# Attention probabilities transposed by VectorE and DMA instead of TensorE, with the attention's instruction order written by hand, in a fused FFN-attention-FFN kernel

## The chip, the cores and the metric

The kernel runs on one core of a Trainium2 chip. The metric is device time in microseconds (us), the median of several runs. Engine names follow the profile: PE is TensorE's matmul side and PEld its weight loads, DVE is VectorE, ACT is ScalarE, POOL is GpSimd, and SP is the engine that issues the DMA transfers.

## The reference

All data are float32. The input `x` is 4 x 256 tokens of 512 features. Three layers are added to it in turn: half of a feed-forward layer of 64 gated low-rank experts, causal attention with 32 heads, and half of the feed-forward layer again. Each sees `x` normalized over its features.

```python
x = x + 0.5 * _L0_ffn_ref(_layernorm(x), A, B, Wr)
x = x + _L0_attn_ref(_layernorm(x), wq, wkv, wo)
x = x + 0.5 * _L0_ffn_ref(_layernorm(x), A, B, Wr)
```

The attention is what the change touches:

```python
q = einsum('bsd,de->bse', hidden, wq).reshape(B, S, 32, 192)
k, v = ...                                  # 32 heads of 128 each, from wkv
scores = einsum('bqhd,bkhd->bhqk', q[..., :128], k) * 192 ** -0.5
probs = softmax(where(causal, scores, -1e30), axis=-1)
attn = einsum('bhqk,bkhd->bqhd', probs, v).reshape(B, S, 32 * 128)
return einsum('bse,ed->bsd', attn, wo)
```

## The kernel before, in words

**Products with fewer multiplications.** Every large product is done by the Strassen-Winograd scheme, the attention's in two levels: an outer split into seven products M1 to M7, and each of these into seven again. Sums of operand blocks are made ahead: those of the weights by POOL (`two_levels`, with `right_sums` at line 187 and the outer sums at lines 588 to 609), those of the tokens once. One stage computes the seven inner products of one or two outer ones (`seven`, with the order in `STEPS`). Inner products M1, M6, M7 and M4 of a stage accumulate in one PSUM bank, M5 and M3 in a second, M2 in a third. After each product DVE or ACT reads the bank and adds it to its place in SBUF; M6 goes into the bank of M1 only when M1 has been read, and so on. Five banks (`ps_mm`) rotate among the stages.

**The attention.** The 32 heads form 16 pairs (`p`). While the units of pair `p` run, PE also computes q and k of pair `p + 1` (`make_qk`: stages a, b, c, d, e of M1, M2 with M6, M4 with M7, M5 and M3; matmuls at line 714, reads at 731 to 765) and part of v (`make_v`, every two pairs one set; matmuls at line 808, reads at 833 to 865). A unit is one head of one batch, so a pair has 8 and the kernel 128. Its work:
- `probs`: two score matmuls (lines 1084, 1085) into the one bank of `ps_s`. Causality leaves three blocks of 128 x 128: the first 128 queries against 128 keys, the second 128 against 256. DVE adds the mask and takes the row's extreme (1093), ACT takes the exponential with its row sum (1104), DVE the reciprocal (1112), and ACT scales (1114).
- `attend`: PE transposes the three blocks against an identity (1125), ACT copies them to SBUF as `pT` (1127), PE multiplies by v (1130, 1137), and ACT copies the result into `attn` (1144).

Unit u's `attend` runs in two halves under the next unit. Strings such as `"qvbqvbq"` (`UNITS`, `FIRST_UNITS`, `LAST_UNITS`) say how many steps of q (`q`), v (`v`), the attend halves (`b`) and the output projection (`o`) a unit takes. In pair 0 PE keeps exactly that order (`manual_schedule` of PE). In later pairs the strings give the order of recording, from which a scheduler of the language derives each engine's order. Which engine waits for what is always handled by semaphores. All DMA transfers are issued by SP, in order.

**Transfers around it.** `load_qk` and `load_v` bring the weights of later pairs in pieces of 128 KB (line 585) into rotating tiles, 7 for q and k and 6 for v. `sum_right` makes the operand sums of `wo` for a pair, `sum_left` those of `attn`; both go to DRAM (`kept_right`, `kept_left`; lines 570, 571, 925, 926). The output projection (`out_products`, 28 steps of 56 matmul instructions at line 1063, two for each product of 128 x 128 x 128) reads them back through tiles of three buffers (946, 956), makes the inner sums on DVE (975), and begins beside the units of the last pair. The second feed-forward layer follows.

Of the kernel before, what the change touches and what calls it, by code (L numbers as in the profile page):

```python
# [13 lines left out]
P = 128  # L14
# [6 lines left out]
HG = 2  # L21
# [11 lines left out]
def macaron_kernel(  # L33
# [16 lines left out]
        tc.tile_pool(name="scratch", bufs=1, space=bass.MemoryType.DRAM)  # L50
    )
# [506 lines left out]
    raw, rights, turns = {}, {}, {}  # L558

    def sum_right(p):  # L560

        w = opool.tile([P, HG, 512], F32, tag="w", name=f"wo_{p}", bufs=1)
        nc.sync.dma_start(w, wo_v[:, p * HG : (p + 1) * HG, :])
        t = opool.tile([P, 3, 256], F32, tag="t", name=f"to_{p}", bufs=1)
        b = [w[:, k, n * 256 : (n + 1) * 256] for k in range(2) for n in range(2)]
        right_sums(nc.gpsimd, [t[:, i, :] for i in range(3)], *b, pinned=True)
        to = kept_right[p // 4][:, p % 4]

        def keep():
            nc.sync.dma_start(to[:, 0], w[:, 0, 256:512])  # L570
            nc.sync.dma_start(to[:, 1:4], t)

        return keep

    def two_levels(pool, bufs, name, blocks, pinned):

        t = {
            m: pool.tile([P, 7, P], F32, tag="w", name=f"{name}_{m}", bufs=bufs)  # L580
            for m in ("M1", "M5", "M2", "M3", "M6", "M4")
        }
        for m, k, n in (("M1", 0, 0), ("M5", 0, 1), ("M2", 1, 0), ("M3", 1, 1)):
            for i, view in enumerate(blocks(k, n)):
                nc.sync.dma_start(t[m][:, i : i + 3 : 2], view)

        def t3():
            return nc.gpsimd.tensor_tensor(t["M1"], t["M6"], t["M1"], ALU.subtract)

        def sums(pinned=pinned):  # L590
            first = nc.gpsimd.tensor_tensor(t["M5"][:, 0:4], t["M5"][:, 0:4], t["M1"][:, 0:4], ALU.subtract)
            if pinned:
                tc.keep_in_program_order(first)

            right = {}

            def inner(m):
                v = t[m]
                right[m] = right_sums(
                    nc.gpsimd, [v[:, i] for i in range(4, 7)], *(v[:, i] for i in range(4))  # L600
                )

            inner("M1")
            inner("M2")
            nc.gpsimd.tensor_tensor(t["M6"][:, 0:4], t["M3"][:, 0:4], t["M5"][:, 0:4], ALU.subtract)
            inner("M6")
            for m in ("M5", "M3"):
                inner(m)
            nc.gpsimd.tensor_tensor(t["M4"], t["M2"], t["M6"], ALU.subtract)

            right["M7"] = right["M1"]
            inner4 = {0: "M1", 1: "M5", 2: "M2", 3: "M3", 4: "M6", 5: "M7", 6: "M4"}
            right["M4"] = {m: t["M4"][:, i] for i, m in inner4.items()}
            return right, t3

        return sums

    def load_qk(p):

        if p < NG:  # L620
            rights["qk", p] = two_levels(
                qkpool,
                7,
                f"wqk_{p}",
                lambda k, n: [
                    view[:, 2 * k : 2 * k + 2, p * HG + n, 0:DN] for view in (wq_v, wk_v)
                ],
                p == 1,
            )()

    def load_v(k):

        if 2 * k < NG:
            raw["v", k] = two_levels(
                vpool,
                6,
                f"wv_{k}",
                lambda c, n: [
                    wv_v[:, 2 * c : 2 * c + 2, (2 * k + n) * HG + j] for j in range(HG)
                ],  # L640
                k == 1,
            )

    def sums_v(k, pinned=False):
        rights["v", k] = raw["v", k](**({"pinned": True} if pinned else {}))
        return rights["v", k]

    with ExitStack() as scope:
# [3 lines left out]
        load_v(0)  # L652
# [6 lines left out]
            aside=lambda: sums_v(0, True),  # L659
# [41 lines left out]
    def make_qk(p):  # L701
        if p >= NG:
            return
        right, t3 = rights["qk", p]
# [63 lines left out]
        if p == 0:  # L768
            turns["qk"] = t3
        yield from stage(("M1",), m1, "a")  # L770
        if p > 0:
            t3()
            yield from stage(("M2", "M6"), onto_copy(slice(0, 4, 3)), "b")
        else:

            yield from stage(("M2",), onto_copy(slice(0, 1)), "n")
            yield from stage(("M6",), onto(base), "o")
        yield from stage(("M4", "M7"), m47, "c")
        yield from stage(("M5",), onto(slice(2, 4)), "d")
        load_qk(p + 1)  # L780
# [13 lines left out]
    def v_stages(k):  # L794
# [3 lines left out]
        right, t3 = rights.get(("v", k)) or sums_v(k)  # L798
        u = 2 + 2 * (k % 2)
        if k == 0:  # L800
            turns["v"] = t3
            t3 = None

# [53 lines left out]
        def m47(part, adds, ps, r):  # L857
# [11 lines left out]
            "M1": stage(("M1",), m1, "a", t3),  # L869
# [10 lines left out]
    def make_v(p):  # L880

        k = p // 2
        if p % 2:
            yield from chain(*(v_by[k + 1][m] for m in ("M2M6", "M4M7") if v_by[k + 1]))
        else:
            yield from v_by[k]["M5"]
            load_v(k + 1)
            v_by[k + 1] = v_stages(k + 1)
            yield from v_by[k]["M3"]
            if v_by[k + 1]:  # L890
                yield from v_by[k + 1]["M1"]
# [14 lines left out]
    def keep_first(p):  # L906

        nc.sync.dma_start(kept_left[p // 4][:, p % 4, 0], attns[p][:, 0, 0:512])
        yield

    def sum_left(p):

        s = hold.tile([P, 3, 512], F32, tag="so", name=f"so_{p}", bufs=1)
# [20 lines left out]
    def out_products(stream):  # L934
# [109 lines left out]
        for _ in sums(0):  # L1044
            pass
# [276 lines left out]
```

## Time and profile before

| what | us |
|---|---|
| median of 3 runs | 1159.51 (1158.92 to 1160.22) |
| the profiled execution's own time | 1158.9 |
| its span, first to last instruction | 1157.1 |

The profile shows one execution. Its span is 1.8 us shorter than that execution's own time. The granted TensorE clock is full (1.0) throughout. A "group" in the profile is all instructions of one line, engine, operation and shape; its row gives the time the engine was busy with it, the mean duration of one in ns, and behind the second bar the idle time just before them and who ended it. A duration runs from start to end of one instruction, and neighbours overlap in the pipeline, so the place that an instruction takes is read from the distance between starts. Some further groups that later steps refer to:

| group | count | mean ns |
|---|---|---|
| PE 1125, transpose of 128 x 128 | 384 | 273 |
| PE 1130 / 1137, products with v, 256 / 128 columns | 256 / 256 | 384 / 274 |
| DVE 1093, mask and extreme, 256 / 128 columns | 128 / 128 | 420 / 290 |
| ACT 1104, exponential, 256 / 128 columns | 128 / 128 | 496 / 402 |
| ACT 1114, scaling, 256 / 128 columns | 128 / 128 | 495 / 403 |
| POOL 187, inner sums of q and k weights, 128 x 128 | 320 | 456 |

By stretches of the span: the first layer runs to about 127 us, projections and the 128 units to about 888 us, the output projection (which begins at 852 us, beside the last pair) to about 1040 us, and the second layer to the end.

### The profile page before, as it was taken

How to read it: one execution, taken by the hardware profiler on the slowest of the kernel's cores; microseconds unless marked ns; L12 is line 12 of the kernel's file. 1: busy time of each engine (PE TensorE's matmuls, PEld its weight loads, DVE VectorE, ACT ScalarE, POOL GpSimd, SP SyncE). 2: the span in 40 equal slices, each digit the busy share in tenths (PEclk: the TensorE clock that was granted, in tenths of full speed). 3: DMA queues.
4: the chain of work that ended last, by engine and by line, in shares of the span. 5: the costliest groups of instructions: out<-in, count | busy, mean ns of one | idle time of the engine just before them, and what ended most of it. 6: DMA issues, size and time to landing. Idle time of an engine off the chain costs nothing.

```text
span 1157.1 us, 20441 instructions
## 1 busy us (share of the span) xinstructions
PE 1147.0 (99%) x7164; PEld 1009.6 (87%) x7164; DVE 756.9 (65%) x2096; ACT 483.5 (42%) x1438; POOL 617.0 (53%) x866
## 2 busy tenths in 40 slices
PE   9999999999999999999999999999999999999998
PEld 6677888899999999999999999999989999995767
DVE  5544776666666667667657767666686887866432
ACT  4444334455555545555555555545553000106410
POOL 4715487778768868768849859858520000001120
PEclk9999999999999999999999999999999999999999
DMA  9101111213233142233233232322386998741001
GB/s 336 69 1 37 44 49 28 82 47 114 99 99 110 56 146 103 62 120 119 68 106 110 93 109 75 127 81 94 137 291 208 364 312 299 252 145 60 19 19 37
DMA packets 107414, 136.73 MB, mean 118 GB/s; under 512 B 7472, under 2 KB 77104, under 8 KB 105136
## 3 DMA queue, kind: packets, MB, share of 16 engines
q1 hardware_dynamic: 107312, 135.43, 34.9%
q8 instruction: 57, 0.93, 0.3%
q14 instruction: 45, 0.37, 0.1%
HBM read 91.36 MB, written 44.04 MB: 117 GB/s over the span
## 4 chain that ended last, share of the span: by engine, by line
PE 95%; DVE 2%; DMA 1%; ACT 1%; issue 0%; SPq 0%; DVEq 0%; ACTq 0%
PE po_M L1063 14%; PE pqk_c L714 8%; PE po_f L418 8%; PE ph_f L350 8%; PE pqk_b L714 8%; PE pa L1130 5%; PE ps L1085 5%; PE pqk_e L714 4%; PE pqk_d L714 4%; PE pv_c L808 4%; PE pqk_a L714 4%; PE pv_b L808 4%; PE ptp L1125 4%; PE pa L1137 2%; PE ps L1084 2%; PE pv_e L808 2%
## 5 line engine op out<-in xcount | busy, mean ns | idle before, releaser
L1104 ACT ACTIVATE s<-s,least 128x128 f32<-128x128 f32 (+1 forms) x256 | 114.8, 449 | 207.0 <-DVE least L1093 207.0
L380 POOL TENSOR_TENSOR hg_f<-hg_f,gate_f 128x512 f32<-128x512 f32 x32 | 33.5, 1058 | 299.9 <-ACT gate_f L305 191.4
L1063 PE MATMUL po_M<-or_M,ol_M 128*128 128x128 f32 x1568 | 178.6, 275 | 1.4 <-DVE or_M L975 1.3
L1063 PEld LDWEIGHTS po_M<-or_M,ol_M 128*128 128x128 f32 x1568 | 177.0, 192 | 2.1 <-DVE or_M L975 1.9
L187 POOL TENSOR_TENSOR wqk_M<-wqk_M 128x128 f32<-128x128 f32 x320 | 137.9, 456 | 9.7
L714 PE MATMUL pqk_c<-xop,wqk_M 128*128 128x256 f32 x448 | 114.4, 380 | 0.1
L1114 ACT ACTIVATE s<-s,arden 128x128 f32<-128x128 f32 (+1 forms) x256 | 102.5, 449 | 13.6 <-DVE arden L1112 12.6
L714 PE MATMUL pqk_b<-xop,wqk_M 128*128 128x256 f32 x420 | 106.3, 379 | 0.0
L731 DVE TENSOR_TENSOR qk<-qk,pqk_b 128x512 f32<-128x512 f32 x105 | 72.2, 688 | 39.8 <-PE pqk_b L714 38.8
L975 DVE TENSOR_TENSOR ol_M<-ol_M 128x512 f32<-128x512 f32 x112 | 77.7, 694 | 21.5 <-DMA ol_M<-left 19.6
L1093 DVE CUSTOM_DVE_ANT_0 s<-ps,mask 128x128 f32<-128x128 f32 (+1 forms) x256 | 81.2, 355 | 12.1 <-PE ps L1085 9.3
L731 DVE TENSOR_TENSOR qk<-qk,pqk_c 128x256 f32<-128x256 f32 (+1 forms) x112 | 59.6, 532 | 42.0 <-PE pqk_c L714 24.9
L714 PEld LDWEIGHTS pqk_c<-xop,wqk_M 128*128 128x128 f32 x448 | 79.2, 191 | 8.5 <-DVE qk L731 0.9
L1144 ACT COPY attn<-pa 128x256 f32<-128x256 f32 x128 | 47.6, 372 | 84.5 <-PE pa L1137 69.7
L731 DVE TENSOR_TENSOR qk<-qk,pqk_d 128x512 f32<-128x512 f32 x112 | 74.7, 684 | 11.8 <-PE pqk_d L714 8.1
L714 PEld LDWEIGHTS pqk_b<-xop,wqk_M 128*128 128x128 f32 x420 | 74.8, 191 | 7.4
L1130 PE MATMUL pa<-pT,vbuf 128*128 128x256 f32 x256 | 77.3, 384 | 0.5 <-ACT pT L1127 0.3
L1085 PE MATMUL ps<-qk 128*128 128x256 f32 x256 | 76.5, 380 | 0.0
L187 POOL TENSOR_TENSOR wv_M<-wv_M 128x128 f32<-128x128 f32 x160 | 69.0, 456 | 11.2 <-DMA wv_M<-in_wkv 4.8
L1127 ACT COPY pT<-ptp 128x384 f32<-128x384 f32 x128 | 60.1, 469 | 29.8 <-PE ptp L1125 28.9
L430 DVE TENSOR_TENSOR x<-x,po_f 128x256 f32<-128x256 f32 x56 | 23.5, 420 | 63.4 <-PE po_f L418 63.3
L714 PE MATMUL pqk_a<-xop,wqk_M 128*128 128x256 f32 x224 | 64.2, 381 | 0.5 <-ACT qk L738 0.5
(191 smaller groups left out, 2576.9 us busy)
## 6 DMA issues: line engine op xcount, KB each, us to landing
ol_M<-left SPq DMA_DIRECT2D x56, 512.0 KB, 5.6
left<-attn SPq DMA_DIRECT2D x15, 1024.0 KB, 3.9
left<-so SPq DMA_DIRECT2D x16, 768.0 KB, 5.1
wv_M<-in_wkv SPq DMA_DIRECT2D x64, 128.0 KB, 2.7
wqk_M<-in_wq SPq DMA_DIRECT2D x64, 128.0 KB, 2.3
wqk_M<-in_wkv SPq DMA_DIRECT2D x64, 128.0 KB, 2.7
wo<-in_wo SPq DMA_DIRECT2D x16, 512.0 KB, 3.9
or_M<-right SPq DMA_DIRECT2D x32, 256.0 KB, 5.7
```

The lines of the kernel that those rows point to most:

```text
L187: pieces = [lambda eng, of=of: eng.tensor_tensor(*of, ALU.subtract) for of in sums]
L350: nc.tensor.matmul(ps, lhsT=left[m][:, c, :], rhs=a_right[m][:, c, :], start=first and c == 0, stop=c == 1, skip_group_check=True,)
L418: nc.tensor.matmul(ps[:, 0:256], lhsT=left[m][:, c, :], rhs=b_right[m][:, c, :], start=first and c == 0, stop=c == 3, skip_group_check=True,)
L714: nc.tensor.matmul(ps[:, i * S : (i + 1) * S], lhsT=right[m][n], rhs=xop[OUTER[m]][:, INNER[n]], start=first and i == 0, stop=True, skip_g ...
L731: nc.vector.tensor_tensor(to, of, ps, ALU.add)
L808: nc.tensor.matmul(ps[:, i * S + t * P : i * S + (t + 1) * P], lhsT=xop[OUTER[m]][:, INNER[n], t * P : (t + 1) * P], rhs=right[m][n], star ...
L1063: nc.tensor.matmul(banks[at // 2][:, cols : cols + P], lhsT=left[n][:, g, t * P : (t + 1) * P], rhs=right[n][:, g], start=k % 4 == 0 and g ...
L1085: nc.tensor.matmul(ps[:, P : 3 * P], lhsT=qT[:, P : 2 * P], rhs=kT, start=True, stop=True)
L1093: nc.vector.tensor_tensor_reduce(out=s[:, cols], in0=ps[:, cols], in1=mask_f[:, cols], scale=-SCALE, scalar=-TAKEN, op0=ALU.add, op1=ALU.m ...
L1104: nc.scalar.activation(s[:, cols], s[:, cols], AF.Exp, bias=least[:, i : i + 1], scale=-1.0, accum_out=den[:, i : i + 1],)
L1114: nc.scalar.mul(s[:, cols], s[:, cols], rden[:, i : i + 1])
L1130: nc.tensor.matmul(po[:, 0 : 2 * P], lhsT=v_of(p, j, 2 * b), rhs=pT[:, 0 : 2 * P], start=True, stop=False,)
```

## The change

**The transposition.** For units 8 to 117 of the 128 the transposes leave PE. ACT writes its scaled probabilities to a PSUM tile `pn` whose columns are grouped so that the 32-column groups k = 0 to 3 of all three blocks lie together. One DVE instruction transposes every 32 x 32 block of it into `pb` in SBUF. That turns the elements inside each block, but each block still lies in the 32 partitions of its queries and not in those of its keys. Four DMA transfers (one per 32 partitions) write the blocks to a DRAM tile `moved`, in runs of 96 elements, and a fifth reads it back as `pT` with the keys in the partitions. The columns of `pT` are then in the order (q, t, c) of 4 x 3 x 32, and `attend` reads its moving operand through a rearranged view, in runs of 32. `attend` comes two units after `probs` (it was one). Pair 0 and the last ten units keep the transposes on PE (`turn`), with ACT's copy.

**The order.** From pair 1 to the end of the units, and for the first 54 of 392 steps of the output projection, the order on PE, DVE, ACT, POOL and SP is the order of recording. `merged` interleaves the steps of q and v in proportion to their PE time, `written` places a unit's parts at marks in estimated PE time, and tables (`Q_SUMS`, `V_SUMS`, `LEFT_SUMS`, `RIGHT_SUMS`, `Q_LOADS`, `V_LOADS`, `LEFT_STORES`) say in which unit which sums and transfers stand. The sums of a pair, made in one go before, are spread over the units. The left stores become seven transfers per pair. The first step of the output projection loads into free tiles of the q and k weights, during pair 14. The buffers of `s` go from 3 to 2.

The core of the diff:

```diff
-    def probs(h, b):
+    def probs(h, b, by_dma=True):
...
         nc.vector.reciprocal(rden, den)
+        if not by_dma:
+            for i, cols in enumerate(parts):
+                nc.scalar.mul(s[:, cols], s[:, cols], rden[:, i : i + 1])
+            pTs[h, b] = s
+            return
+        pn = ps_t.tile([P, 4, 3, 32], F32, tag="pt", name=f"pn_{n}")
         for i, cols in enumerate(parts):
-            nc.scalar.mul(s[:, cols], s[:, cols], rden[:, i : i + 1])
-        return s
...
+            nc.scalar.mul(
+                pn[:, :, i : 2 * i + 1, :].rearrange("p k t c -> p t k c"),
+                s[:, cols].rearrange("p (t k c) -> p t k c", k=4, c=32),
+                rden[:, i : i + 1],
+            )
+        yield
+        pb = work.tile([P, 4, 96], F32, tag="pb", name=f"pb_{n}", bufs=1)
+        nc.vector.transpose(pb.rearrange("p k c -> p (k c)"), pn.rearrange("p k t c -> p (k t c)"))
+        moved = turning.tile([P, 4, 96], F32, tag="moved", name=f"moved_{n}")
+        for q in range(4):
+            nc.sync.dma_start(
+                moved[:, q].rearrange("(k r) x -> r k x", r=32), pb[32 * q : 32 * q + 32]
+            )
+        yield
+        pT = pTs[h, b] = work.tile([P, 4, 3, 32], F32, tag="pT", name=f"pT_{n}")
+        nc.sync.dma_start(pT.rearrange("p q t c -> p (q t c)"), moved.rearrange("p q x -> p (q x)"))
...
+    def attend(h, b):
...
+        of = pTs.pop((h, b)).rearrange("p q t c -> p t q c")
...
-            rhs=pT[:, 0 : 2 * P],
+            rhs=of[:, 0:2],
...
-            rhs=pT[:, 2 * P : 3 * P],
+            rhs=of[:, 2:3],
...
+    ENGINES = {EngineType.PE, EngineType.DVE, EngineType.Activation, EngineType.Pool, EngineType.SP}
...
+    def classic(number):
+
+        return number < 8 or number >= 8 * NG - 10
+
+    def written(p, unit, steps, streams, transfers):
+
+        number = 8 * p + unit
+        made = probs(*units[number], not classic(number))
+        next(made)
+        todo = sums_of(p, unit)
+        t, done, n = 0.65, 0, len(todo)
+
+        marks = [(1.3, made), (1.9, pending.pop(0)), (2.0, transfers), (2.8, made)]
+        if not classic(number):
+            marks.append((4.2, made))
+        if not classic(number - 2):
+            marks.append((2.1, units[number - 2]))
+        if classic(number - 1):
+            marks += [(1.0, ("turn", *units[number - 1])), (2.2, units[number - 1])]
...
+        for i, (k, cost) in enumerate(steps):
+            take(streams[k], 1)
+            t += cost
+            while done < n and (done + 0.5) / n <= (i + 1) / len(steps):
+                todo[done]()
+                done += 1
+            while marks and marks[0][0] <= t:
+                t += mark(marks.pop(0)[1])
...
+            written_out.enter_context(tc.manual_schedule(engines=ENGINES))
```

The marks read: exponentials (1.3), the fifth transfer of the unit before (1.9), other transfers (2.0), `attend` of the unit two back (2.1), reciprocal and scaling (2.8), block transpose and four writes (4.2), in us of PE time from the unit's start; the score matmuls and DVE's reductions stand at its head.

## The prediction

> **What bounds the kernel now.** I read the page from the top: busy time by engine, then the chain that ended last.
>
> ```profile
> PE 1147.0 (99%) x7164; PEld 1009.6 (87%) x7164; DVE 756.9 (65%) x2096; ACT 483.5 (42%) x1438; POOL 617.0 (53%) x866
> ...
> PE 95%; DVE 2%; DMA 1%; ACT 1%; issue 0%; SPq 0%; DVEq 0%; ACTq 0%
> ```
>
> TensorE is busy for 99% of the span and carries 95% of the chain. A busy engine can hide waits, so I asked for the busy time in the stretch that the change rewrites, from the first projection products (127.6 us) to the end of pair 14.
>
> ```profile
> 127.60:836.00 708.40, 705.97 (x4399) 642.62 (x4398) 482.26 (x1346) 356.05 (x1137) 532.23 (x762) 1.00 0.28 92
> ```
>
> The columns are length, then busy time with instruction count of PE, PEld, DVE, ACT and POOL, then granted clock, DMA share and GB/s. PE is idle for 2.4 us of 708.4; DVE is busy 68%, ACT 50%, POOL 75%, DMA 28%. The transpose matmuls of line 1125 start between 153.3 and 885.8 us, one group per unit, so a unit (one head of one batch) takes 732.5/127 = 5.77 us on average. Work taken from PE here shortens the kernel one for one, unless something takes the freed place.
>
> **What is removed from PE.** The timeline of PE shows what the three transposes of a unit cost:
>
> ```profile
> 245.73 0.49 PE L1125 MATMUL ptp<-ident,s 128*128 128x128 f32 x3
> 246.06 1.06 PE L808 MATMUL pv_c<-wv_M,xop 128*128 128x128 f32 x8
> ```
>
> They look 0.49 us long, but the next matmul starts 0.33 us after the first one, so their place is 0.33 us. (The group's 63.0 us for 384 counts pipeline ends that lie under the next matmul.) Units 8 to 117 go by DMA, 110 of 128; pair 0 and the last ten keep the transposes. Gain: 110 x 0.33 = 36.3 us. Against the profiled execution of 1158.9 us (span 1157.1) that leaves 1122.6 us. The other matmuls stay the same in number and shape, but `attend` now reads its moving operand in runs of 32 columns. No row has such an operand. Low end 0; high end one more 128x128 pitch (0.11 us, a third of the 0.33) for each of 220 matmuls, 24 us. I take 0, because all contiguous rows move at the same rate per column and the run is still 128 bytes.
>
> **VectorE.** 110 block transposes of 128x384 are added.
>
> ```profile
> L731 DVE TENSOR_TENSOR qk<-qk,pqk_d 128x512 f32<-128x512 f32 x112 | 74.7, 684 | 11.8 <-PE pqk_d L714 8.1 <-POOL wqk_M L187 0.8 <-POOL qk L765 0.3
> L731 DVE TENSOR_TENSOR qk<-qk,pqk_e 128x256 f32<-128x256 f32 x112 | 45.4, 417 | 14.8 <-PE pqk_e L714 12.2
> L1127 ACT COPY pT<-ptp 128x384 f32<-128x384 f32 x128 | 60.1, 469 | 29.8 <-PE ptp L1125 28.9
> ```
>
> By the two DVE rows 128 columns cost (684 - 417)/2 = 134 ns, so 384 columns take 0.55 us, 0.47 back to back (such operations follow each other about 80 ns before the listed end). Low end 0.42 (the 256 row), high end 0.95 (two cycles per element). I take 0.47: 52 us of DVE. Per unit DVE has 3.93 us (68% of 5.77) and then 4.40 of 5.44, or 81%. ACT loses the 0.47 us copy and keeps its two scalings; POOL keeps 4.34 us per unit, or 80%. None becomes the bound on average.
>
> The average is not the limit, though. PSUM banks tie PE to DVE closely: in a stage of seven products, M1, M6, M7 and M4 use one bank, so the product after next waits until DVE has read the one before (`STEPS`). DVE runs in order, and two new waits stand in its hand-written order: the reciprocal behind ACT's exponentials (it was placed by the scheduler before) and the transpose behind ACT's scaling. Behind a waiting transpose are queued the reads of the next products, and PE waits for those within about one product, 0.43 to 0.86 us. The worst place is stage d (M5), where each product of 0.43 us brings a 128x512 read of 0.60. I counted the DVE order of the changed kernel in such a unit: two reductions 0.56, six reads of d at 0.60, reciprocal 0.1, transpose 0.47, one read of e 0.34: 5.07 us, beside PE's 7 x 0.43 + 2 x 0.44 + 2 x 0.65 = 5.2. It just fits, with nothing left for a wait on ACT. Low end of these waits 0; high end 0.7 us in each of the 28 such units, 20 us. I take 0.2 us in each: 6 us. They belong to the hand-written order as a whole; its other moves (sums spread over POOL, earlier loads) I cost at nothing, since POOL has 20% free. If that cover is gone, PE waits for weight sums directly.
>
> **SP and the DMA engines.** Each of the 110 units issues five more transfers: four writes of 32 partitions (128 runs of 384 bytes each) and one read of 128 rows of 1536 bytes. The left stores are also cut from two transfers per pair to seven.
>
> ```profile
> 532.50:538.50 6.00, 6.00 (x42) 5.59 (x41) 3.33 (x11) 3.74 (x13) 4.36 (x8) 1.00 0.49 134
> ```
>
> In this window six weight loads of 128 KB ran, each 256 runs of 512 bytes: 0.49 x 6.0 x 16 engines = 47 engine-us for 1536 runs, 31 ns a run. A unit's 512 written runs then take 512 x 31/16 = 1.0 us of all engines, the read about 128 x 61/16 = 0.5 us (61 ns for 1536 bytes, from 40 ns a KB in the window of the left stores at 542 to 551 us, where the share is 0.51). So the share rises from 28% by 1.5/5.44 = 28% to some 58%. Here the Trainium skill speaks against the change. "DMA: Bandwidth & Descriptors", Rules for kernel authors, says to transpose by the hardware's DMA transpose and not by a plain transfer with a rearranged pattern, which is 19 times slower; its Specifications say that below 512 bytes an engine reads, modifies and writes. By the first, the unit's 196 KB (0.7 us at the window's 134/0.49 = 273 GB/s) would take 14 us, far over the unit, and the kernel some 2000 us. I don't take it: VectorE has turned the elements already, and DMA only moves whole runs of 96. By the second the writes may double to 2.0 us and the share reach 76%, still under the unit. No run of before writes so short a run. I take the row, and the doubled price as the high end.
>
> The SP queue matters more, because it waits in order. The read of a unit waits on SP until its four writes have landed, and behind it stand the next unit's weight loads and left stores, and the next four writes. From the rows:
>
> ```profile
> right<-wo SPq DMA_DIRECT2D x16, 128.0 KB, 1.8
> ...
> 515.90 0.34 SPq L570 DMA_DIRECT2D right<-wo  x1
> ...
> 532.69 0.37 SPq L585 DMA_DIRECT2D wqk_M<-in_wq  x1
> 533.15 1.96 SPq L585 DMA_DIRECT2D wv_M<-in_wkv  x4
> ```
>
> The round is three issues at 0.34, then 1.8 us from the last issue to its landing (the nearest row: 128 runs to DRAM), the read's issue 0.38, and 22 other transfers per pair, 2.75 per unit at 0.44 = 1.2: in all 4.4 us of 5.44. Latency: from the transpose (4.2 to 4.9 us into unit n) about 1.0 + 1.8 + 0.2 + 2.6 (the landing of the small weight loads) = 5.6 us; the matmul that needs it stands 2.1 us into unit n + 2, some 7.5 us later. There are about 2 us to spare. Units with six or seven other transfers overrun by up to 1 us and get it back in the next. So I cost the round at nothing. Nobody else waits on it except ACT, through the `attn` buffer that a late left store keeps.
>
> **Last pair.** It stays as it was in kind, and its loads must still come: PE idled 1.7 us of 46 in 844 to 890, and after that has no idle time to lose although DMA is at 0.97. I take no change, within 3 us either way.
>
> **The rivals.**
> A, the likeliest: 1158.9 - 36.3 + 6 = 1128.6 us; with the 0.6 us by which the median of before lies over its profiled run, 1129. For it: 2.4 us of idle PE before, and room on every engine. Its own range is 1120 to 1137.
> B, VectorE's in-order waits cost more: 0.7 us in the 28 stage d units (20 us) and 0.05 us in all 110 (5 us), no more than is within reach of the 0.95 us price of a transpose. 1122.6 + 25 = 1148 us. For it: DVE at 97% of the unit in stage d. Against: before, at 68% load, PE stood only 0.6 us for reads of d.
> C, slower: the SP round. Place: the read's wait in SP for the writes' landing. If a short write lands in 3.5 us and not 1.8, the round is 6.1 us, PE waits for each pT, and 110 x (6.1 - 5.44) = 73 us come back: 1196 us. The point from which it decides: above 5.44 us a round it eats the gain, above 5.77 (landing over 3.1 us) the kernel is slower. For it: left<-attn landed in 3.9 us, and short writes may be dearer. Against: those were 1 MB, and the 128 KB store took 1.8.
> D, the gain is eaten in full: POOL, ordered by hand, delivers weight sums late; stage b, about 7 us into a pair, needs M6's sums, whose loads land some 3 us into the pair and then take 4.9 us. A delay of 2.6 us in each of 14 pairs gives 1159. Against: the first products of b need none of the inner sums.
>
> **How the numbers follow.** A 0.58, B 0.21, C 0.17, D 0.04. The predicted time is A's, 1129. The range takes in A and B with the uncertain ends, 1120 to 1158, and leaves out C, D and a little. Within 0.2% (about what a measurement of this kernel can tell from no change) lies D alone. A and B are faster, 0.79; D 0.04; C 0.17.
>
> **What would show it.** Right: PE instructions fewer by 330, PE still at 98% or more between 196 and the last pair, a unit of about 5.45 us, DVE near 80% there, waits of pqk_d and pqk_e products on DVE of some 6 us in all, almost none of the pa products on pT's load. Each block transpose should take 0.5 to 0.6 us. Wrong by C: pa products waiting for DMA in nearly every unit, and moved landing in over 3 us. Wrong by B: DVE waiting for ACT's pn, with PE waiting for DVE in the units of stage d. Wrong by D: pqk_b waiting for POOL. What would break the sum altogether: matmuls of pa that take longer than 379 and 274 ns.

## The result and the profile after

The changed kernel takes 1201.28 us in the median of 4 runs (1196.65 to 1207.47), the kernel before 1159.22 us in runs on the same chip (1158.72 to 1160.22). The ratio is 1.037, with a 95% interval of 1.032 to 1.041: slower by 42 us, where 1129 us was forecast. The profiled execution of the changed kernel took 1196.65 us, its span 1194.8 us.

The page of the kernel after, busy time by engine and then the chain that ended last:

```profile
PE 1133.5 (95%) x6834; PEld 981.5 (82%) x6834; DVE 792.3 (66%) x2230; ACT 443.6 (37%) x1328; POOL 619.5 (52%) x866
...
PE 34%; DMA 2%; DVE 2%; POOL 1%; SPq 1%; issue 1%; ACT 1%; DVEq 0%; POOLq 0%; ACTq 0%
```

TensorE (PE) lost the 330 instructions as planned (7164 to 6834), but it is idle for 61.3 us where it was idle for 10.1. The shares of the chain add up to under half, so I take from it only that DMA and SyncE's queue (SPq) have more of it than before. The rewritten stretch, from the first projection products to the end of pair 14, in the same columns as in the prediction (length, busy time of PE, PEld, DVE, ACT and POOL, granted clock, DMA share, GB/s):

```profile
128.00:866.00 738.00, 686.22 (x4058) 609.75 (x4057) 512.55 (x1454) 316.54 (x1029) 530.81 (x761) 0.99 0.51 144
```

PE is idle for 51.8 us of 738, where 2.4 of 708.4 were idle. No other engine is near full: DVE 69%, ACT 43%, POOL 72%, DMA 51%. Who PE waits for is in the list of its waits (us in total, times, longest):

```profile
PE pa L1234 <- DMA pT<-moved: 23.6, 16, 2.7
PE pqk_e L729 <- DVE qk L746: 13.8, 11, 2.1
PE pqk_d L729 <- DVE qk L746: 6.1, 13, 0.6
PE pv_b L821 <- POOL wv_M L610: 3.1, 5, 1.2
PE pqk_e L729 <- POOL vbuf L878: 2.8, 3, 0.9
```

The first row is the new transfer, the next two are reads of stages d and e. The groups that were added or priced in the prediction (by shape: line, engine, tiles, count, busy us, mean ns, then idle time before and its releaser):

```profile
L746 DVE TENSOR_TENSOR qk<-qk,pqk_d 128x512 f32<-128x512 f32 x112 | 73.0, 678 | 2.9 <-PE pqk_d L729 1.7 <-POOL wqk_M L610 0.2
...
L1203 DVE STREAM_TRANSPOSE pb<-pn 128x384 f32<-128x384 f32 x110 | 63.5, 578 | 40.2 <-DMA moved<-pb 37.6 <-ACT qk L753 2.3 <-ACT pn L1196 0.3
```

A block transpose takes 578 ns, as sized (0.55). Idle before it, 37.6 us, is DVE waiting until the writes out of the one `pb` buffer have landed. The transfers, with the median time from issue to landing, and what SyncE waited for:

```profile
moved<-pb SPq DMA_DIRECT2D x440, 48.0 KB, 2.3
pT<-moved SPq DMA_DIRECT2D x110, 192.0 KB, 2.5
```

```profile
SPq L1211 <- DMA moved<-pb: 171.5, 180, 3.2
```

In total, for 171.5 us a read of `pT` stood at the head of SyncE's queue and waited for the writes, and everything behind it waited too. How that looks in one unit of pair 7, first SyncE's queue, then PE:

```profile
568.31 0.34 SPq L1211 DMA_DIRECT2D pT<-moved  x1
568.70 2.99 SPq L607 DMA_DIRECT2D wv_M<-in_wkv  x6
571.73 0.47 SPq L950 DMA_DIRECT2D left<-attn  x1
572.30 1.90 SPq L1206 DMA_DIRECT2D moved<-pb  x4
576.04 0.34 SPq L1211 DMA_DIRECT2D pT<-moved  x1
```

```profile
575.72 0.61 PE L821 MATMUL pv_a<-wv_M,xop 128*128 128x128 f32 x4
578.72 0.67 PE L1234 MATMUL pa<-pT,vbuf 128*128 128x256 f32 x2 [2.39 <-DMA pT<-moved]
579.23 0.38 PE L1241 MATMUL pa<-pT,vbuf 128*128 128x128 f32 x2
579.45 1.62 PE L729 MATMUL pqk_c<-xop,wqk_M 128*128 128x256 f32 x4
```

The reads stand 7.73 us apart: seven other issues take 3.4 us, the four writes 1.9, then SyncE does nothing from 574.20 to 576.04 until the last write has landed. The read lands about 2.5 us later, and the product that needs it starts 2.39 us late. The four `pqk_c` products after it take 1.62 us where the same four took 1.03 at 574.85 us; that is the clock (last section).

### The profile page after: what moved, and what is told of

Its sections match the earlier page's. It is cut to its first block, busy times and chain, and to the rows that moved or that the text cites. A ratio compares the mean times of both kernels' runs of the same rounds, so it can differ in the third digit from the quotient of the medians.

```text
span 1194.8 us, 21108 instructions
## 1 busy us (share of the span) xinstructions
PE 1133.5 (95%) x6834; PEld 981.5 (82%) x6834; DVE 792.3 (66%) x2230; ACT 443.6 (37%) x1328; POOL 619.5 (52%) x866
## 5 line engine op out<-in xcount | busy, mean ns | idle before, releaser
L1134 PE MATMUL po_M<-or_M,ol_M 128*128 128x128 f32 x1512 | 172.3, 275 | 0.0
L1134 PEld LDWEIGHTS po_M<-or_M,ol_M 128*128 128x128 f32 x1512 | 171.0, 192 | 0.3
L610 POOL TENSOR_TENSOR wqk_M<-wqk_M 128x128 f32<-128x128 f32 x320 | 141.0, 456 | 12.1
L610 POOL TENSOR_TENSOR wqk_M<-wqk_M,wqk_M 128x512 f32<-128x512 f32 (+1 forms) x64 | 107.1, 1682 | 30.5 <-DMA wqk_M<-in_wkv 14.9
L1234 PE MATMUL pa<-pT,vbuf 128*128 128x256 f32 x256 | 78.8, 389 | 25.5 <-DMA pT<-moved 23.6
L1196 ACT ACTIVATE pn<-s,arden 128x128 f32<-128x128 f32 x220 | 93.8, 427 | 11.6 <-DVE arden L1188 7.5
L610 POOL TENSOR_TENSOR wv_M<-wv_M,wv_M 128x512 f32<-128x512 f32 (+1 forms) x32 | 53.8, 1680 | 76.2 <-DMA moved<-pb 32.5
L1203 DVE STREAM_TRANSPOSE pb<-pn 128x384 f32<-128x384 f32 x110 | 63.5, 578 | 40.2 <-DMA moved<-pb 37.6
L1037 DVE TENSOR_TENSOR ol_M<-ol_M 128x512 f32<-128x512 f32 (+1 forms) x112 | 74.6, 666 | 19.1 <-DMA ol_M<-left 16.5
L729 PE MATMUL pqk_e<-xop,wqk_M 128*128 128x256 f32 x224 | 64.8, 395 | 16.7 <-DVE qk L746 13.8
L780 POOL TENSOR_TENSOR qk<-qk 128x256 f32<-128x256 f32 x64 | 46.4, 727 | 58.4 <-DVE qk L746 58.3
```

The lines of the kernel that those rows point to most:

```text
L610: return nc.gpsimd.tensor_tensor(to, a, b, ALU.subtract)
L729: nc.tensor.matmul(ps[:, i * S : (i + 1) * S], lhsT=right[m][n], rhs=xop[OUTER[m]][:, INNER[n]], start=first and i == 0, stop=True, skip_g ...
L1037: nc.vector.tensor_tensor(of[:, :, to], of[:, :, a], of[:, :, b], op)
L1134: nc.tensor.matmul(banks[at // 2][:, cols : cols + P], lhsT=lhsT, rhs=rhs, start=k % 4 == 0 and g == 0 and at % 2 == 0 and t == 0, stop=Tr ...
L1196: nc.scalar.mul(pn[:, :, i : 2 * i + 1, :].rearrange("p k t c -> p t k c"), s[:, cols].rearrange("p (t k c) -> p t k c", k=4, c=32), rden[ ...
L1203: nc.vector.transpose(pb.rearrange("p k c -> p (k c)"), pn.rearrange("p k t c -> p (k t c)"))
```

## The experiments

**How the loss is divided.** The forecast less its 6 us for DVE is a span of 1157.1 - 36.3 = 1120.8 us. The starts of the projection's stage a tell where each kernel is later than that. Lengths of a pair in us, mean over pairs 2 to 13, worked out from the traces (the forecast row is the one of before less 8 x 0.33):

| kernel | even pairs | odd pairs |
|---|---|---|
| before | 43.9 | 47.0 |
| forecast with no new wait | 41.3 | 44.4 |
| after | 46.8 | 49.3 |
| e1 loads first | 46.3 | 46.7 |
| e3 no move | 41.9 | 46.6 |
| e4 order only | 44.6 | 48.7 |
| e7 spread | 44.1 | 46.8 |
| e10 best | 42.3 | 45.8 |

**The two halves of the change.** e4 keeps the written order and leaves all transposes on TensorE; e3 keeps the transposes on DVE and leaves out the five transfers.

```diff
 # e4
-        return number < 8 or number >= 8 * NG - 10
+        return True
 # e3
-        pb = work.tile([P, 4, 96], F32, tag="pb", name=f"pb_{n}", bufs=1)
+        pb = work.tile([P, 4, 96], F32, tag="pT", name=f"pb_{n}")
-        moved = turning.tile([P, 4, 96], F32, tag="moved", name=f"moved_{n}")
...
-        nc.sync.dma_start(pT.rearrange("p q t c -> p (q t c)"), moved.rearrange("p q x -> p (q x)"))
+        pTs[h, b] = pb.rearrange("p q (t c) -> p q t c", t=3)
```

> The changed kernel with the transposes on PE in all units, so only the order written by hand and the moved loads and sums remain. If the order costs nothing: 1156 to 1164 us, with PE idle of about 10 us as before. If the order costs waits of its own: 1170 us or more. SP's rounds do not exist here; both theories on the transfers say nothing.

> The changed kernel without the five transfers of a unit: VectorE's block transpose writes straight into pT and attend reads that, so the blocks are left in their queries' partitions. The output projection and all else stays. Left out: the move of the blocks between partitions. It measures the block transposes and the hand-written order alone. If SP's round and the transfers cause the whole loss: 1122 to 1135 us (36.3 us saved on PE, few waits). If VectorE's load or the order written by hand causes a good part of it: over 1150 us.

e4 took 1180.54 us (ratio 1.018, 1.017 to 1.020), e3 1145.68 (0.9885, 0.987 to 0.990). The written order alone costs 21 us; and e3, which leaves out the move of the blocks between partitions and so has none of its transfers, is 23 us above the 1122.6 of the sum. So this part of the loss does not need the transfers. That the two amounts agree does not show that they have one cause. PE's waits in stages d and e are 8.8 us in e4 and 14.0 in e3 (0.6 in the kernel before), first e4, then e3:

```profile
PE pqk_d L729 <- DVE qk L746: 5.3, 10, 0.6
PE pqk_e L729 <- DVE qk L746: 3.5, 8, 0.5
```

```profile
PE pqk_d L729 <- DVE qk L746: 7.2, 16, 0.6
PE pqk_e L729 <- POOL vbuf L878: 5.7, 6, 0.9
PE pqk_e L729 <- DVE qk L746: 1.1, 2, 0.9
```

The row with POOL is a wait for DVE too. At 524.86 us, for example, PE starts when DVE's read of `pqk_e` has ended (524.75), and that read stood behind a read that had waited 0.88 us for ACT's copy and behind the block transpose (523.83 to 524.41).

The rest, from e3 to the changed kernel (1194.8 - 1145.4 = 49.4 us of span, 55.6 by the medians), belongs to the transfers.

**The transfers: order of the issues.** e1 issues the other transfers of a unit before the read, so that the writes land under them; e2 gives `pb` a second buffer (and `s` one in place of two, for the space).

```diff
 # e1
-        marks = [(1.3, made), (1.9, pending.pop(0)), (2.0, transfers), (2.8, made)]
+        marks = [(1.3, made), (1.9, transfers), (2.0, pending.pop(0)), (2.8, made)]
 # e2
-        pb = work.tile([P, 4, 96], F32, tag="pb", name=f"pb_{n}", bufs=1)
+        pb = work.tile([P, 4, 96], F32, tag="pb", name=f"pb_{n}", bufs=2)
```

> The changed kernel with two marks exchanged: in each unit SP issues the weight loads and left stores (1.9) ahead of the read of pT (2.0). The theory is that SP's round per unit is the bound: four writes, wait for their landing, read, other transfers, 5.97 us from one read of pT to the next where PE needs 5.44. With this order the other transfers are issued while the writes land, about 1.26 us a unit comes off the round, which falls to some 4.7 us, below PE's unit. Then the waits of pa for pT and of DVE for pb go, and the kernel takes 1125 to 1145 us. The rival that the DMA engines themselves are too slow for these short runs, or that the hand-written order is at fault, expects 1185 to 1205 us, because neither the transfers nor the other engines' orders change.

> The changed kernel with two buffers of pb, at the cost of one of s (the units with transposes on PE keep their s in the pb buffers). It takes away DVE's 37.6 us of waiting for the landing of moved. If the SP round is the bound, the lateness only moves: pa waits longer for pT, the distance of the reads stays near 5.9 us, and the time stays at 1185 to 1205 us. If the loss comes from DVE standing behind a single buffer (in-order waits on DVE), the PE waits for reads of stages d and e (20 us) and their clock loss go, and it takes 1165 to 1175 us.

e1: 1176.11 us (1.015, 1.014 to 1.017), 25 us gained by exchanging two marks. e2: 1199.48 (1.035, 1.033 to 1.038): the buffer is not the cause, the lateness only moves (PE's wait for `pT` rises from 23.6 to 33.4 us). In e1 the odd pairs are as long as in e3 (46.7 and 46.6 us), so there the transfers cost nothing any more; the even ones lose 4.4 us each, and those are the pairs with one unit of seven and one of six other transfers.

e7b leaves the queue as it is and gives each round 2.5 us more time before its product; e7 exchanges the marks as e1 does, spreads the loads so that no unit has more than five other transfers, and has the later product too.

```diff
 # e7b and e7
-            marks.append((2.1, units[number - 2]))
+            marks.append((4.6, units[number - 2]))
 # e7 alone, besides the edit of e1
-    Q_LOADS = {6: ("M1", "M5"), 7: ("M2", "M3")}
-    V_LOADS = {3: ("M1", "M5", "M2"), 6: ("M3",)}
+    Q_LOADS = {5: ("M1",), 6: ("M5",), 7: ("M2", "M3")}
+    V_LOADS = {2: ("M1",), 3: ("M5",), 4: ("M2",), 6: ("M3",)}
```

> The changed kernel with one edit: the product pa of a unit stands at 4.6 us in the second unit after it instead of 2.1, so each transfer round has 2.5 us more. Theory that only the latency of single rounds with six or seven other transfers was too long: 1148 to 1160, pa waits nearly gone. Rival, that SyncE's rounds are on the average longer than a unit (5.97 us measured against 5.44), so that any slack is used up and lateness accumulates: 1185 to 1200, pa waits 15 us or more.

> Three edits that leave all work as it is: the other transfers ahead of the read (as e1), the weight loads spread so that no unit has more than five other transfers instead of seven, and pa at 4.6 us. If SyncE's bursts are all that e1 still loses over e3 (its even pairs lose about 4 us each at pa, the odd ones none): 1144 to 1152 us, no waits of pa on pT. If the transfers' own contention costs as well: 1155 to 1170.

e7b took 1207.06 us (1.041, 1.039 to 1.042). The wait for `pT` has all but gone, and the time has not. PE's waits in e7b:

```profile
PE pqk_d L729 <- DVE qk L746: 14.8, 17, 2.1
PE pqk_e L729 <- DVE qk L746: 12.3, 11, 2.7
PE pv_b L821 <- POOL wv_M L610: 7.3, 6, 1.8
PE pqk_a L729 <- POOL wqk_M L610: 6.9, 6, 1.2
...
PE pa L1234 <- DMA pT<-moved: 2.4, 6, 0.4
```

So it is the rate of SyncE's rounds, not their latency: with more time they take it through other doors, DVE waiting for `pb` (48.7 us) and POOL for late weights. The rate must be read with care. There is one read of `pT` per unit, so the distance of the reads is the length of a unit in every version, whatever holds it up (5.97 us in the changed kernel, 6.06 in e7b, 5.50 in e10). What tells is the round without the time in which SyncE stands at the writes until DVE has made the block transpose. Worked out from the traces, it is 5.46 us in the changed kernel and 5.32 in e7b, with nothing to spare against the forecast's unit of 5.44, but 4.13 in e1 and 4.12 in e10. In 59 of the changed kernel's 109 rounds SyncE goes on to the writes within 0.15 us.

e7, where the rate is mended, took 1160.00 us (1.000, 0.999 to 1.001), 47 us below e7b, but outside the 1144 to 1152 expected if bursts were all that was left. Of the 14 us by which it lies above e3, 5.9 are waits for `pT`, and PE's wait of `pqk_a` for ACT rose by 5.5 (0.7 to 6.2). That second wait is as long in e7b, which has only the later product, so the later product has a price of its own.

**The written order: the scheduler back.** e5, e5a, e5b and e5d take engines out of the set whose order is written by hand.

```diff
-    ENGINES = {EngineType.PE, EngineType.DVE, EngineType.Activation, EngineType.Pool, EngineType.SP}
+    ENGINES = {EngineType.PE, EngineType.SP}
 # e5 with e4's edit; e5b alone; e5d with e1's edit
+    ENGINES = {EngineType.PE, EngineType.DVE, EngineType.Pool, EngineType.SP}
 # e5a, with e4's edit
```

> All transposes on TensorE as in e4, and only TensorE's and SyncE's order written by hand; VectorE, ScalarE and GpSimd are ordered by the scheduler again. Theory (the hand order of the three vector engines makes VectorE late in stages d and e and costs some 20 us): 1159 to 1164 us, pqk_d and pqk_e waits on DVE under 3 us. Rival 1 (TensorE's new order, the placing of scores, turns and products among the projection steps, is what costs): 1178 to 1183, as e4. Rival 2 (SyncE's order of the ordinary transfers makes POOL's sums late): 1175 or more with the waits on POOL and wqk/wv tiles.

> As e4 (all transposes on TensorE, order by hand), except that ScalarE alone is ordered by the scheduler. If the cost of the hand order is that ScalarE's copies of stage c stand behind scalings and exponentials, and VectorE waits for them in order (qk of line 746 on ACT line 777, 65.5 us in e4, 16.1 in the kernel before): 1159 to 1166, that wait back near 20 us. If VectorE's own order is to blame (its reads stand behind the softmax rows and the reciprocal): 1176 to 1182.

> The changed kernel with only TensorE's and SyncE's order by hand, the vector engines ordered by the scheduler. If the two costs add (about 22 us for the order of the vector engines, about 55 us for SyncE's round of transfers): 1176 to 1184 us, the waits of pa on pT still 20 us or more. If SyncE's round hides what the vector engines lose, so that they don't add: 1195 to 1203. If the late round was itself a result of late vector engines (the transpose comes late, so its writes do): under 1160.

> As e1 (the other transfers of a unit issued before the read of pT, so that the writes' landing is hidden behind them) with the vector engines ordered by the scheduler. If the costs add: 1176 less 22, 1150 to 1158 us. If what is left in e1 is the wait of SyncE for VectorE's transpose (113.1 us there) and the scheduler's order shortens it: 1135 to 1150. If the round of transfers alone decides: 1172 to 1178, as e1.

All four missed: 1207.75 us (1.041, 1.040 to 1.043), 1200.31 (1.035, 1.034 to 1.037), 1311.38 (1.129, 1.126 to 1.132) and 1274.66 (1.099, 1.097 to 1.101). My theory that VectorE's, ScalarE's and GpSimd's written orders cost some 20 us, which the scheduler would give back, fell. The waits of d and e are still there (pqk_d 9.8 us and pqk_e 2.7 in e5, 5.3 and 3.5 in e5a, 5.3 and 3.5 in e4), and new ones for ScalarE's copy of `pT` come on top: 8.1 us in e5, 2.9 in e5a. The list shows less than is lost there, because a wait shorter than the overlap of two matmuls (379 ns from start to end, 216 from start to start) leaves no idle time. By the distances of PE's starts in pairs 2 to 13, the products with v come 17 us later in all than in e4, in e5 and in e5a alike. In this order of recording, which puts a product with v 1.2 us behind its transposes, the scheduler's choice is worse than the written one. With the transfers it is far worse: in e5b a unit takes 7.07 us and PE waits 78.8 us for `pT`.

**The written order: stages d and e.** e6 puts exponential, scaling and block transpose later in e3's order. e9 makes the copies of stage c on DVE, so that DVE need not wait for them. e12 puts e4's transposes and products with v where the kernel before had them.

```diff
 # e6, on e3 (with the block transpose at 4.6 in place of 4.2)
-        marks = [(1.3, made), (1.9, pending.pop(0)), (2.0, transfers), (2.8, made)]
+        marks = [(2.1, made), (1.9, pending.pop(0)), (2.0, transfers), (3.2, made)]
 # e9, on e3 (and the same for vbuf)
-                nc.scalar.copy(part(one, r), ps[:, 0:1])
+                nc.vector.tensor_copy(part(one, r), ps[:, 0:1])
 # e12, on e4
-            marks += [(1.0, ("turn", *units[number - 1])), (2.2, units[number - 1])]
+            marks += [(1.95, ("turn", *units[number - 1])), (3.25, units[number - 1])]
```

> As e3 (no five transfers; it leaves out moving the blocks between partitions), but the exponentials, the scaling and the block transpose of a unit stand later in the written order, at 2.1, 3.2 and 4.6 us instead of 1.3, 2.8 and 4.2. Theory for the 22 us that e3 lies above 1122.6: ScalarE reaches the exponential before VectorE has reduced the scores, waits there in order, and the copy of stage c behind it comes late, so VectorE waits for that copy (511.98 us in e3: 1.31 us) and enters stage d late. With the exponential later the copy goes ahead of the wait: 1128 to 1138 us, pqk_d waits under half of 7.2 us. Rival 1: VectorE has simply too much work in stages d and e: 1143 to 1147, waits as before. Rival 2: the later softmax makes pa late: over 1150, waits of pa on the transpose.

> As e3 (no five transfers; leaves out moving the blocks between partitions), but the copies of stage c that ScalarE made (88 in the stretch, qk and vbuf) are made by VectorE itself, so that VectorE no longer waits for them in its order. VectorE gets 88 times 0.34 us, 30 us more work. If the in-order waits for ScalarE's copies make VectorE late in stages d and e: 1128 to 1138 us against 1145.7, and the waits of pqk_d and pqk_e fall to a third. If VectorE's own load there is the cause: 1146 to 1155, waits as before or more.

> As e4 (all transposes on TensorE, everything ordered by hand, 1180.5 us), with TensorE's transposes at 1.95 us of a unit and the products with v at 3.25, where the kernel before had them, instead of 1.0 and 2.2. If the place of these steps makes VectorE and ScalarE late in stages d and e: 1160 to 1168 us. If it is the rest of the written order (where VectorE's reads and ScalarE's copies stand among the softmax): 1176 to 1182, with only the waits of ptp and pa (5.7 us in e4) gone.

e6 took 1158.48 us (0.999, 0.998 to 1.000), 13 us more than e3: PE's waits of pqk_d rose from 7.2 to 8.2 us, those of pqk_e stayed (6.8, both rows above, and 6.6), and 6.5 us of pqk_a behind ACT came in place of 0.7. Its theory fell; DVE waited for ACT's copies of `qk` 57.9 us, hardly less than in e3 (62.1). e9 took 1142.56 us (0.985, 0.983 to 0.986), 3 us less than e3 and between its two forecasts: the waits for these copies are gone altogether, and nearly all of the loss stays. Why, is to be seen in stage d of one odd pair. The windows run from the first product of d to the first of e, in the kernel before, e4, e3 and e9:

```profile
521.29:527.79 6.50, 6.50 (x44) 5.79 (x43) 5.75 (x14) 2.91 (x9) 6.42 (x12) 1.00 0.28 90
```

```profile
528.71:536.00 7.29, 6.69 (x42) 5.80 (x41) 5.66 (x14) 3.96 (x12) 6.45 (x13) 1.00 0.32 108
```

```profile
511.09:518.06 6.97, 6.35 (x39) 5.52 (x38) 6.08 (x16) 3.41 (x11) 6.81 (x13) 1.00 0.33 114
```

```profile
509.40:516.35 6.95, 6.36 (x39) 5.55 (x38) 6.75 (x18) 2.69 (x8) 6.45 (x13) 1.00 0.36 116
```

The fourth and fifth numbers are PE's and DVE's busy time. Before, PE had no idle time beside a DVE that was busy 5.75 us of 6.50. In e4 DVE does the same amount, 5.66 us, but PE is idle 0.60: DVE has free time there, at the wrong moments. In e3, with the block transposes, it is busy 6.08 us and PE idle 0.62. In e9 DVE is busy 6.75 us of 6.95, 97%, and PE is idle 0.59 all the same: its waits are gone, but with the copies that it took over DVE is itself full in this stage. The other odd pairs from 3 to 13 show the same within 0.03 us. So both are true, in different versions, and taking away either uncovers the other.

e12 took 1174.75 us (1.013, 1.011 to 1.014), 6 us less than e4. The d and e waits almost vanished (pqk_d 1.0 us and pqk_e 1.5), so the place of those steps among the products is one cause. 15 us stay: 1.3 us before the first pair, 8 in the pairs, and 7 from pair 14 on, where one wait of a transpose for ACT takes 4.2 us. Of the 8 in the pairs the list of waits shows little, again because they are short. By the distances of PE's starts in pairs 2 to 13, 4.6 us of 7.2 stand before products with v: such a product comes 0.25 us after the projection product ahead of it, where before it was 0.22.

**Put together.** e8 is e7 with e6's later marks and the product at 4.8; e11 also gives d more time by other weights in `merged`; e10 is e8 with e9's copies; e13 is e10's order with all transposes on TensorE.

```diff
 # e11
-            of_v = at[2] < len(v) and (at[0] == len(q) or at[3] / total[1] < at[1] / total[0])
+            of_v = at[2] < len(v) and (at[0] == len(q) or at[3] / total[1] < at[1] / 21.77)
-            at[i + 1] += cost
+            at[i + 1] += cost if of_v else (0.36, 0.8, 0.8, 0.65, 0.5)[(at[0] - 1) // 7]
 # e13, on e10
-        return number < 8 or number >= 8 * NG - 10
+        return True
```

> e7 and the later exponential, scaling and transpose of e6 together (2.1, 3.2, 4.6 us; pa at 4.8). If both costs are independent and both theories hold: 1128 to 1142 us, faster than the kernel before. If e6's edit does nothing: 1144 to 1152. If the later block transpose makes the transfers late again: over 1155 with waits of pa on pT.

> As e8, with one edit in the merging of the two product streams: a step of stage d counts 0.65 and one of e 0.5 where both counted 0.43, a counts 0.36 and b and c 0.8, so that more of the v products stand between the products of d and e. If VectorE's work per TensorE time in d and e makes the waits: 1143 to 1149 us. If entering d late is all that counts: 1151 to 1153.

> As e8 (all work done, 1152.1 us), with stage c's copies by VectorE as in e9. If the copies are the cause and the two causes add: 1134 to 1145. If VectorE's load is the cause: 1152 to 1162, the block transposes and so the transfers later.

> As e10 (1145.4 us), but all transposes on TensorE and no transfers for them. If the transposition by VectorE and DMA is worth its 36.3 us on TensorE once the transfers are hidden: 1175 to 1182. If the block transposes on VectorE (97% busy in stage d of e9 and e10) eat part of the gain: 1160 to 1172. If the mended order alone made e10 fast: 1145 to 1155.

e8: 1152.11 us (0.994, 0.992 to 0.995). The later marks, which cost 13 us in e3, gain 8 here; I can't say why, the marks act on each other. e11: 1154.01 (0.995, 0.993 to 0.996), no gain. e10: 1145.41 us (0.987, 0.986 to 0.989), at the edge of what was expected if the two gains add, and faster than both kernels. e13: 1179.87 (1.018, 1.016 to 1.019). PE's waits in e10:

```profile
PE pqk_d L729 <- DVE qk L746: 3.7, 11, 0.7
PE pqk_d L729 <- DVE arden L1188: 3.5, 6, 0.6
PE pqk_e L729 <- DVE qk L746: 3.3, 8, 0.5
PE ptp L1220 <- ACT s L1191: 2.1, 1, 2.1
PE pa L1234 <- DMA pT<-moved: 2.1, 5, 0.8
```

All five transfers of each of these units run in e10, and PE waits 2.1 us for them in all. Between e10 and e13 lie 34.5 us, close to the 36.3 that the transposes take on TensorE. So, in this order, the exchange itself is worth what it was said to be worth, once SyncE's queue is in order.

## Why the prediction was wrong

Against the forecast's span (1128.6 - 1.8 = 1126.8 us) the changed kernel is 68.0 us late in its profiled execution, the fastest of the four. The spans divide that: 49.4 us for the transfers (after less e3); 24.6 us for the written order (e3 less 1120.8), of which 6 had been counted. 49.4 + 24.6 - 6 = 68.0.

- **The gain on TensorE, 36.3 us, was right**: 330 instructions fewer, 34.5 us between e10 and e13. So were the strided operand at nothing (`pa` products 379 and 275 ns in the median, before 379 and 274), the block transpose (578 ns for 0.55 us), and the DMA share. The stretch has 0.51 x 738 = 376 us of all engines' time for 0.28 x 708 = 198 before; the difference by 110 is 1.6 us a unit, for the 1.5 that I had. By their parts two errors cancelled: a packet of 384 bytes took 26.5 ns in the mean where I had 31, one of 1536 bytes 89 where I had 61 (from the trace, within the stretch). The two rules of the Trainium skill, "DMA: Bandwidth & Descriptors", which I had weighed and set aside, are not seen here: 19 times slower would have been 14 us a unit, my estimate from that factor, and runs of 384 bytes at twice the price would have made 2.5 us; a 512-byte packet of the same stretch took 29.7 ns, more than the shorter one.
- **The step that failed: "So I cost the round at nothing."** The round was counted at 4.4 us of 5.44. Measured, it takes 5.97 us in the mean, of which 5.46 are SyncE's own. A unit of e3, which has no such round, takes 5.53 us (its two rows above, by 16), and 110 x (5.97 - 5.53) = 48 us is the size of the transfers' loss. The terms: four writes and their landing, counted 1.0 + 1.8 = 2.8 us, take 3.67 (an issue 0.43 to 0.47 us where I took 0.34 from one row, though the line under it shows four in 1.96; and 1.66 us from the last issue's end to the last landing); the other transfers were right (2.66 a unit at 0.44 = 1.17). What I left out is some 0.6 us a unit in which SyncE stands at the writes until DVE has made the block transpose. And "units with six or seven other transfers overrun by up to 1 us and get it back in the next" was wrong at both ends. By the number of other transfers between two reads, the mean distance is 4.84 us with none, 5.31 with one, 5.65 with two, 6.05 with four and 7.66 with six or seven: those overrun by 2.2 us, and an average unit has nothing to give back. Number is not all: the seven rounds with three others take 7.61 us. Six of them have two stores of 256 KB and the 512 KB load of `wo` just ahead of the writes, and there the last write lands after 3.1 to 4.3 us, where the means of the other groups are 1.9 to 2.4.

    This is rival C in place and kind, at 5.97 where its example had 6.1; but its reason, a short write that lands in 3.5 us, holds in those six rounds only. The median write lands in 2.3. That C's 1196 us is so near to the measured time is luck: it had 73 us for the round and none for the order, and the runs show some 49 and 25.
- **VectorE's waits, "I take 0.2 us in each: 6 us", were too small by a factor of four.** e3 loses 24.6 us, which is near rival B's 25, but not all of it is B's: PE's listed waits in d and e are 14.0 us there (22.7 in the changed kernel, with its row of POOL), and 6 us stand behind the start of pair 14 (next point). B's wait is seen: DVE waiting for ACT, and reads behind the block transpose, with PE idle. Yet e4, which has no block transpose, loses 22 us of span. The count of 5.07 us of DVE beside 5.2 us of PE in stage d told that there was no room, and I took a low value between 0 and 20 all the same. B was no alternative to C, either: both happened, and I had given B and C one chance each as if they excluded one another.
- **"Last pair: I take no change, within 3 us either way."** From the start of pair 14 the kernel before needs 350.2 us, e3 354.1, e4 354.8 and the changed kernel 357.9. With the 2.0 us that e3 should have gained there, that is 6 us of its 24.6.
- **Rival D** was seen only as a consequence: `pqk_b` waits for no sums, and `pv_b` 3.1 us for v's weights, a wait which e3 and e1 do not have: with the round taken away or mended, the weights come in time.

Where the loss of the order stands can be told. In pairs 2 to 13 e3 is 16.7 us over the forecast; by the distances of PE's starts 8.8 of it stand before products of stage d, 6.0 of stage e and 2.7 of stage a, which is all of it within 1 us.

What stays open: how the 22 us of the written order divide by cause between the places of PE's steps (e12 moved 6), DVE's waits in its order, and its load in stage d (e9 took 3 and found DVE full). No version has lost all of it; e10 still lies 23 us over 1122.6.

## What to carry to other kernels

Here the transfer that reads back what others have written made the issuing queue wait for their landing, and every transfer behind it waited too. In such a case count that queue as an engine with a busy time for each round (issues, landing, and its wait for the producer), unit by unit, and put it beside the unit's length; if it does not fit, put other issues between the write and the read, and spread the bursts (e7: 47 us under e7b). Before an order is written out by hand, run it alone without the feature it is made for: e4 would have shown 21 us of cost before the first transfer was written.

## What the runs showed of the hardware that was not expected

A wait of TensorE of 2.39 us was enough to halve its clock, because of where it lay. The windows below (columns as above) are the 3.41 us in which that wait falls and the 3.41 us behind them:

```profile
576.33:579.74 3.41, 1.02 (x6) 0.97 (x7) 2.42 (x9) 1.33 (x6) 3.41 (x5) 1.00 0.72 224
579.74:583.15 3.41, 3.41 (x13) 2.97 (x12) 1.54 (x4) 1.40 (x4) 3.33 (x8) 0.50 0.42 99
```

The granted clock is 0.50 in the second, and the four products of 579.45 us, most of which fall in it, take 1.62 us for 1.03. The trace has five such stretches between 313 and 887 us, each 3.413 us long. Their starts lie 266.2, 13.7, 273.1 and 17.1 us apart, which is 78, 4, 80 and 5 times 3.413, so in this run the clock goes by a fixed grid of windows. The five windows just before them had 1.8 to 2.6 us of idle PE. Waits of 2.54 us at 673.69 and 2.53 us at 769.84 lost no clock: a border of that grid cuts each, and no window has more than 1.6 us of it. The idle time that decides is not sharp in these traces: a window with 2.0 us of it, at 491 us, was not followed by a slow one. The Trainium skill, "TensorE: Matmul & The Clock Gate", Part 1, gives half speed after at least one idle window of about 3.4 us. The length agrees; but here a window that was idle for little more than half did it.

Over the whole span the clock is 0.993, some 8 us. e3 loses 1.7 us in the same way, so up to a seventh of what the transfers cost is clock and not wait. In e10, with waits of at most 0.8 us for the transfers, it is 1.000.

The landing of a small write goes with what is issued just ahead of it. The same 48 KB writes land in 2.3 us (median) in the changed kernel and in 1.7 in e1 and e10, where they follow the read and the loads stand behind them. Within the changed kernel, the 28 writes of rounds with no other transfer land in 1.7 us too (median), the others in 2.3 to 2.6, by the transfer that stands ahead of the four.
